# Sending each token's row to its two experts alone in a fused attention and mixture-of-experts kernel

## The chip, the cores and the metric

The kernel runs on one core of one Trainium2 chip. The metric is the device time of one execution in microseconds (us), the median of three runs; lower is better. One further execution was recorded by the hardware profiler, and all durations of single instructions come from that one. The engines are TensorE (PE in the profile; its weight loads are PEld), VectorE (DVE), ScalarE (ACT), GpSimd (POOL) and SyncE (SP). SP only issues transfers; GpSimd issues some too.

## The reference

One transformer layer on x of 2 x 2048 tokens by 512 features, in float32: attention with 16 query heads of 32 and a single key and value head, a residual and a layer norm; then a mixture of 8 experts of which each token uses 2, a residual and a layer norm.

```python
q, k, v = split(x @ Wqkv.T + b)              # q: 16 heads of 32; k and v: one head of 32
scores = q @ k.T / sqrt(32), causal mask     # 2048 x 2048 per head and batch
ctx = softmax(scores) @ v
x1 = layernorm(x + ctx @ Wout.T + b_out)

s = x1 @ router_w.T                          # 8 scores for a token
top, sel = top_k(s, 2);  g = softmax(top)    # two experts, two shares
h = silu(x1_bf16 @ w1[sel]) * (x1_bf16 @ w3[sel])     # 512 -> 128, for the two chosen
out = layernorm(x1 + sum over the two of g * (h @ w2[sel]))   # 128 -> 512
```

## The kernel before, in words

**Tiles and stages.** The 4096 tokens are 32 tiles of 128, in 8 groups of 4 tiles (`TG`), 16 tiles for each batch row. `project` turns the four x tiles of a group on TensorE, makes keys and values (`keys`) and queries (`queries`) in float32. `attention` goes through the tiles in turn; a tile T has as many steps as there are key tiles up to and with its own: 1 to 16, 272 in all. Each step is one score block, four matmuls of 512 columns into the PSUM tile `three` and one loose bank; ACT takes the exponential into `pT` (into `acc` for the tile's own, diagonal block); TensorE multiplies by the values into `cs` (`weigh`); and VectorE adds `pT` to `acc` for the softmax sums (`add_up`). The diagonal block is masked by GpSimd (`affine_select` in `exponentials`) before `weigh` uses it as its second block. `after` ends a tile: sums, the output projection with `woT`, the residual `xr` and a layer norm, of which VectorE does the statistics and GpSimd three small operations (`layernorm`, L692).

**Experts.** `experts` (L781) treats four tiles of a group together, except in the last group, whose tiles go alone. For each tile `route` turns x1 on TensorE and casts it to bf16 on GpSimd (`x1b`); `gates` makes the scores, the two best by `max` and `max_index`, and a gate of 8 numbers per token, zero but for two. Then every token goes through all eight experts: `up` and `half` do 8 matmuls each of 512 columns against `w1_sb` and `w3_sb` (in two halves of four experts), ACT takes a tanh, VectorE a product, GpSimd multiplies by the gate, VectorE multiplies into `h`; a transposing DMA on SP's queue turns `h` into `hT`; `down` does 8 matmuls of 512 columns against `w2_sb`. So a tile has 24 matmuls of 512 columns in bf16. The sum is added to x1, normalized and stored.

**What sets the order.** A planner in the kernel (`Order`, L65 on) runs when the program is built. Every piece of work is a `step` with an engine, an assumed duration, a list of buffers that it takes, marks that it waits for, and a priority or a due time. `run` picks, for the engine that can start first, the step of least priority number; scores have 0, `weigh` 1, and steps with a `Due` run at 2 or more until their due time nears. The instructions are then written in the planned order, and on the chip each engine goes through its own list in order, waiting on semaphores. Where real durations differ from the assumed ones, an engine waits at the head of its list. GpSimd's list holds the masks, the residual's bias, the layer norms and the gate products; SP's the loads of x for `project` (`xg`) and for the residual (`xr`), the transposes and the stores.

**Buffers.** Each kind of tile has a ring of its own: 3 `pT`, 2 `acc`, 4 groups of x1 (`X1B`), 2 each of `a`, `h`, `hT`, `xr`, `c_sb`, 1 each of `lT`, `ctxT`. Four loose PSUM banks serve all other matmuls.

**The end.** After all tiles a flag is read: if a softmax sum is out of bounds, the whole computation is done again by a safer form (`run(True)`). With these inputs the flag is 0.

Of the kernel before, what the change touches and what calls it, by code (L numbers as in the profile page):

```python
# [28 lines left out]
X1B = 4  # L29
# [5 lines left out]
BANK = "m"  # L35

# [23 lines left out]
class Order:  # L60
# [5 lines left out]
    LOOK = {DVE: 1.0}  # L66
    CAP = 3.0

    def __init__(self, banks, **rings):
        self.rings = {name: [n, []] for name, n in rings.items()}  # L70
        self.banks = [None] * banks
        self.busy = {e: 0.0 for e in self.LAT}
        self.sig = {}
        self.parked = []
        self.now = self.end = 0.0
        self.event = 0
        self.count = 0
        self.dues = []
        self.held = {}
# [23 lines left out]
    def hold(self, ring, n):  # L103
        self.held[ring] = [self.take(ring) for _ in range(n)]
# [6 lines left out]
    def take_all(self, rings, t):  # L111
        slots = self.slots(rings.count(BANK), t)
        tokens = []
        for ring in rings:
            if ring == BANK:
                token = Token(ring)
                token.slot = slots.pop(0)
                self.banks[token.slot] = token
# [5 lines left out]
    def slots(self, n, t):  # L124

        free = [i for i, k in enumerate(self.banks) if k is None or k.at is not None and k.at <= t + 1e-6]
        free.sort(key=lambda i: self.banks[i].at if self.banks[i] else 0.0)
        return free[:n]

    def room(self, rings):  # L130

        at = 0.0
        n = rings.count(BANK)
        if n:
            free = sorted(0.0 if k is None else k.at for k in self.banks if k is None or k.at is not None)
            if len(free) < n:
                return None
            at = free[n - 1]
        for i, ring in enumerate(rings):
            if ring == BANK:  # L140
                continue
# [30 lines left out]
    def run(self):  # L172
        while self.parked:
# [23 lines left out]
            if eng in self.LOOK and best[1][0].us > 1.0 and self.prio(best[1][0], urgent) > -0.9:  # L197

                for x in able:
                    s = x[1][0]  # L200
                    if (
                        s.eng == eng and self.prio(s, urgent) <= -0.9 and x[0] < t0 + self.LOOK[eng]
# [31 lines left out]
def mqa_postln_moe_postln(  # L234
# [22 lines left out]
    EB = 4  # L257
    scale = 1.0 / math.sqrt(HD)
# [26 lines left out]
    )  # L285
    warm = const.tile([P, 1], F32, name="warm")
# [17 lines left out]

    def run(full):
# [5 lines left out]
        n_x1 = X1B - full  # L311
        x1p = es.enter_context(tc.tile_pool(name="x1p", bufs=n_x1))
        att = es.enter_context(tc.tile_pool(name="att", bufs=1))
        ptp = es.enter_context(tc.tile_pool(name="pt", bufs=3))
# [5 lines left out]
        if full:  # L320
# [19 lines left out]

        order = Order(
            NB, three=1, pT=3, acc=2, cs=1, c_sb=2, lT=1, ctxT=1, shT=3 if full else NSH, pmax=2, xg=1, xT=1,
            xr=2, qT=2, kv=GPB + 1, x1=n_x1, x1b=1, x1T=TG, a=2, h=2, hT=2,
# [18 lines left out]
        banks = [psm.tile([P, GT], F32, name=f"bank{i}") for i in range(NB)]  # L362

        def bank(m, dtype=F32, shape=(P, GT)):
            ap = banks[m.slot][:, :]
# [10 lines left out]
        def score_banks(ms):  # L376

            if len(ms) == NG:
                of = [heads(bank(m)) for m in ms]
                return of, [([m], slice(g, g + 1), of[g][:, None]) for g, m in enumerate(ms)]  # L380
# [9 lines left out]
        def load_weights():  # L390
            nat["wkv"] = ffn.tile([2 * HD, D], F32, tag="a", name="wkv_n")
            nat["wq"] = grp.tile([P, NHH, D], F32, tag="qT", name="wq_n", bufs=2)
            nat["wo"] = grp.tile([P, NHH, D], F32, tag="qT", name="wo_n", bufs=2)
            nat["wr"] = ffn.tile([E, D], F32, tag="a", name="wr_n")
            b_row = nat["b"] = ffn.tile([1, D + 2 * HD], F32, tag="x1T", name="b_row", bufs=TG)
# [7 lines left out]
        def turn_biases():  # L403
# [23 lines left out]
            free(order.held["x1T"][0])  # L427
# [45 lines left out]


        kT, v, qTs, kv_held, qT_held, st_x = {}, {}, {}, {}, {}, {}

        def load_x(G):
            b, gi = divmod(G, GPB)
            xg = grp.tile([P, TG, D], F32, tag="xg", name="xg")
            for t in range(TG):  # L480
                s0 = gi * GT + t * P
                nc.sync.dma_start(xg[:, t, :], x[b, s0 : s0 + P, :])
            return xg

        def project(G, due):
            hurry = -1.5 if G == 0 else None
            due = Due(due, 21.7)
            (hx,) = yield step(SP, 0.0, ["xg"])
            xg = load_x(G)
            st = {}  # L490

            def turn(t):
# [737 lines left out]
```

The helper that records every operation has one line, L230, so most rows of the profile carry that line and are told apart by the names of their tiles.

## Time and profile before

| | us |
|---|---|
| median of three runs | 1216.54 |
| the three runs | 1216.75, 1216.47, 1216.54 |
| the profiled execution: its own time | 1216.7 |
| its span, first to last instruction | 1214.9 |
| VectorE's adds acc<-acc,pT (238) | 549.3 |
| ACT's exponentials pT<-three (240) | 370.1 |
| GpSimd's gate products a<-a,gt (56) | 121.4 |
| granted TensorE clock, mean | 0.992 of full |

"Busy" is the time in which at least one instruction of an engine ran. Matmuls are pipelined, so the mean duration of one is longer than the distance to the next. In a row of a group stand the line, the engine, the operation, output<-inputs by tile names, the shapes, the count, the busy time and the mean of one in ns, then the idle time of that engine just before them and what ended it. A float32 matmul shows as two records. Engine queues that issue transfers are named SPq or POOLq.

### The profile page before, as it was taken

To read this page: it belongs to the slowest core of one execution; us is meant where nothing else is said; L and a number is where in the kernel's file an instruction comes from. 1 tells how busy PE (TensorE), PEld (TensorE's weight loads), DVE (VectorE), ACT (ScalarE), POOL (GpSimd) and SP (SyncE) were. 2 spreads that over 40 slices of the span, in tenths; PEclk is the share of its full clock that TensorE was granted. 3 is DMA by queue.
4 is the path that set the end of the run, shared out by engine and by line. 5 is a ranking of instruction groups with operands and counts; after the bars stand their busy time and mean duration, and the time that the engine had idled before them with its cause. 6 is when DMAs were issued, how large, how long until landed. Compare 5 with 4: busy or idle time off the path is not lost. (4 is left out here: it accounts for less than half of the span.)

```text
span 1214.9 us, 16833 instructions
## 1 busy us (share of the span) xinstructions
PE 1151.1 (95%) x6774; PEld 370.4 (30%) x6774; DVE 910.7 (75%) x1107; ACT 696.2 (57%) x777; POOL 601.5 (50%) x355
## 2 busy tenths in 40 slices
PE   8999999999999999989999999999899899999984
PEld 5433223323222332222333223222232232232341
DVE  2348777778777898787738867868799788879774
ACT  2445666657665676556535666666657567566420
POOL 3244533424363654567544545432765687467542
PEclk9999999999999999999999999999999999999998
DMA  9201001001100201100001000000010010010121
GB/s 248 69 10 52 10 9 44 10 9 44 27 9 24 64 10 27 36 26 18 28 18 60 27 9 18 9 10 9 18 44 28 18 44 19 26 36 18 36 44 56
DMA packets 57354, 40.13 MB, mean 33 GB/s; under 512 B 42729, under 2 KB 43753, under 8 KB 57266
## 3 DMA queue, kind: packets, MB, share of 16 engines
q1 hardware_dynamic: 47248, 34.63, 10.2%
q0 software_dynamic: 9360, 3.15, 2.3%
q8 instruction: 55, 0.90, 0.3%
q10 hardware_dynamic: 658, 1.18, 0.3%
q14 instruction: 33, 0.27, 0.1%
HBM read 25.58 MB, written 8.39 MB: 28 GB/s over the span
## 5 line engine op out<-in xcount | busy, mean ns | idle before, releaser
L230 DVE TENSOR_TENSOR acc<-acc,pT 128x2048 f32<-128x2048 f32 x238 | 549.3, 2308 | 43.5 <-PE cs L230 30.4
L230 ACT ACTIVATE pT<-three,bias 128x1536 f32<-128x1536 f32 x240 | 370.1, 1542 | 325.1 <-PE bank L230 282.3
L230 PE MATMUL bank<-qT,kT_g 32*128 32x512 f32 (+1 forms) x672 | 319.2, 596 | 6.0 <-DVE h L230 4.8
L230 PE MATMUL three<-qT,kT_g 32*128 32x512 f32 x1632 | 310.2, 643 | 10.0 <-ACT pT L230 8.2
L230 POOL TENSOR_SCALAR r<-mv 128x1 f32<-128x1 f32 x64 | 82.5, 1288 | 407.6 <-DVE mv L230 403.7
L230 PE MATMUL cs<-pT,v_g 128*32 128x512 f32 x1920 | 257.9, 608 | 0.2 <-ACT pT L230 0.2
L230 POOL TENSOR_TENSOR a<-a,gt 128x512 f32<-128x512 f32 x56 | 121.4, 2171 | 97.9 <-DVE a L230 97.8
L230 POOL TENSOR_SCALAR x<-x,mv,r 128x512 f32<-128x512 f32 x62 | 166.5, 2685 | 6.8
L230 ACT ACTIVATE pT<-bank,bias 128x512 f32<-128x512 f32 x240 | 163.5, 681 | 0.6 <-PE bank L230 0.6
L230 PE MATMUL bank<-w_sb,x1b 128*128 128x512 bf16 x512 | 125.7, 382 | 9.0 <-DVE h L230 8.2
L230 PEld LDWEIGHTS three<-qT,kT_g 32*128 32x128 f32 x1632 | 83.2, 183 | 163.6 <-ACT pT L230 86.1
L230 PE MATMUL bank<-xT,wqT 128*128 128x512 f32 x256 | 129.2, 621 | 0.0
L230 PE MATMUL bank<-woT,ctxT 128*128 128x512 f32 x256 | 126.1, 613 | 2.5 <-DVE ctxT L230 2.5
L230 POOL TENSOR_SCALAR_AFFINE_SELECT acc<-acc 128x2048 f32<-128x2048 f32 x32 | 68.6, 2145 | 72.1 <-ACT acc L230 72.1
L230 PEld LDWEIGHTS cs<-pT,v_g 128*32 128x32 f32 x1920 | 38.2, 108 | 174.7 <-issue 168.8
L230 POOL TENSOR_TENSOR r<-r,neg_half 128x1 f32<-128x1 f32 x64 | 86.1, 1345 | 5.3
L230 ACT ACTIVATE acc<-three,bias 128x1536 f32<-128x1536 f32 x32 | 49.4, 1543 | 67.8 <-PE three L230 44.4
L230 DVE TENSOR_TENSOR h<-bank,a 128x512 bf16<-128x512 f32 x56 | 38.6, 690 | 59.6 <-POOL a L230 59.6
L230 PEld LDWEIGHTS bank<-qT,kT_g 32*128 32x128 f32 x544 | 79.7, 183 | 8.1 <-DVE h L230 4.1
L230 PEld LDWEIGHTS <-x1b 128*128 128x128 bf16 x512 | 45.5, 98 | 108.0 <-issue 62.0
L230 PE MATMUL bank<-w_sb,hT 128*128 128x512 bf16 x256 | 64.3, 387 | 5.1 <-DMA hT<-h 4.7
L230 PEld LDWEIGHTS bank<-woT,ctxT 128*128 128x128 f32 x256 | 44.2, 189 | 78.8 <-issue 64.7
(109 smaller groups left out, 931.9 us busy)
## 6 DMA issues: line engine op xcount, KB each, us to landing
xg<-in_L_attn_x_dram SPq DMA_DIRECT2D x32, 256.0 KB, 3.8
xr<-in_L_attn_x_dram SPq DMA_DIRECT2D x32, 256.0 KB, 2.7
out_dram<-x SPq DMA_DIRECT2D x32, 256.0 KB, 2.0
w_sb<-in_L_ffn_w_dram POOLq DMA_DIRECT2D x8, 256.0 KB, 8.9
wq_n<-in_L_attn_Wqkv_w_dram ACTq DMA_DIRECT2D x4, 256.0 KB, 6.0
wo_n<-in_L_attn_out_w_dram SPq DMA_DIRECT2D x1, 1024.0 KB
w_sb<-in_L_ffn_w_dram POOLq DMA_DIRECT2D x1, 1024.0 KB, 14.9
hT<-h SPq DMA_TRANSPOSE x31, 3.0
```

Source lines behind the costliest of these rows:

```text
L230: return lambda *a, **k: self.tc.keep_in_program_order(getattr(self.engine, name)(*a, **k))
```

## The change

Seven of the eight groups leave the dense expert block. Their tokens are taken in four sets (two groups, two groups, two groups, one group). For each set there is room in DRAM for 448 rows per expert (256 in the last set).

- `choose(G)` scores a group's tokens as before, then counts with matmuls against ones and a triangle which place each token has in the list of each of its two experts, and writes places and shares.
- `scatter(T)`: two indexed DMAs from GpSimd's queue write a tile's 128 normalized rows, cast to bf16, to their places in `x_by`. Places never written hold zeros, filled at the start by four DMAs from the same queue.
- `expert_set`: for each expert a transposing DMA on SP loads its 448 (or 256) rows; `expert` multiplies with the weights as the fixed operand and the tokens as the moving one; `down` multiplies blocks of 128 rows by `w2_sb`, ACT copies the result out of PSUM and SP stores it in `y_by`.
- `combine` and `second`: x1 is loaded back from DRAM, two indexed DMAs on GpSimd's queue gather each token's two rows of y, VectorE adds them with their shares, and the layer norm follows.
- The last entry of each set in `SETS` gives the attention steps between which the set's experts are planned.
- The last group keeps the dense block, tile by tile.
- Many rings become one pool of 20 pages of 128 x 512 float32 (`PAGES`), with a limit for each kind; `pT` has 5 buffers in place of 3; x of the projection is loaded tile by tile; the four loose banks are one PSUM tile.
- The planner may keep TensorE from starting a lesser step of over 0.5 us if a score step could start within 0.25 us (`LOOK`).
- The flag also covers the counts: if an expert has more tokens than its room, the whole is done again by the safer form, which is dense.

```diff
-X1B = 4
+PAGES = 20
+PT = 5
+X1 = 6
+SETS = (
+    ((0, 1), (448,), (59, 149)), ((2, 3), (448,), (150, 202)), ((4, 5), (448,), (190, 241)),
+    ((6,), (256,), (227, 264)),
+)
...
-    LOOK = {DVE: 1.0}
+    LOOK = {DVE: 1.0, PE: 0.25}
...
+            first_ = 0.0 if eng == PE else -0.9
+            if eng in self.LOOK and best[1][0].us > (0.5 if eng == PE else 1.0) and self.prio(best[1][0], urgent) > -0.9:
...
+                        s.eng == eng and (s.prio == 0.0 if eng == PE else self.prio(s, urgent) <= -0.9) and x[0] < t0 + self.LOOK[eng]
...
+    x_by = [dram.tile([E * n, D], BF16, name=f"x_by{i}") for i, n in enumerate(room)]
+    y_by = [dram.tile([E * n, D], F32, name=f"y_by{i}") for i, n in enumerate(room)]
+    x1_d = dram.tile([NT * P, D], F32, name="x1_d")
...
-        ptp = es.enter_context(tc.tile_pool(name="pt", bufs=3))
+        ptp = es.enter_context(tc.tile_pool(name="pt", bufs=3 if full else PT))
...
         order = Order(
-            NB, three=1, pT=3, acc=2, cs=1, c_sb=2, lT=1, ctxT=1, shT=3 if full else NSH, pmax=2, xg=1, xT=1,
-            xr=2, qT=2, kv=GPB + 1, x1=n_x1, x1b=1, x1T=TG, a=2, h=2, hT=2,
+            NB, PAGES, dict(
+                x1=n_x1, xg=TG, xr=2, lT=1, ctxT=1, c_sb=2, x1T=TG, a=2, h=2, hT=2, y=4, back=9,
+            ),
+            three=1, pT=3 if full else PT, acc=2, cs=1, shT=3 if full else NSH, pmax=2, xT=1,
+            qT=2, kv=GPB + 1, x1b=2, hc=2,
         )
...
             gps.dma_start(w2_sb, w2.rearrange("e p d -> p e d"))
+            for places_ in x_by:
+                k = places_.shape[0] // P
+                gps.dma_start(
+                    places_[:, :].rearrange("(p k) d -> p k d", p=P),
+                    zeros[:, None, :].to_broadcast([P, k, D]),
+                )
...
             mark("ln", T)
             alone = G == NGRP - 1
-            if alone or t == TG - 1:
+            if G in set_of and not full:
+                yield step(SP, 0.0)
+                nc.sync.dma_start(x1_d[T * P : (T + 1) * P, :], y)
+                if t == TG - 1:
+                    spawn(choose(G))
+            elif alone or t == TG - 1:
...
+        def choose(G):
...
+            (m,) = yield step(PE, 0.5, ["m"], due=due)
+            p_n = bank(m, F32, (P, TG + 1, E))
+            flat = p_n.rearrange("p t e -> p (t e)")
+            mm(
+                p_n[:, : TG + 1, :], ones_b, both[:, TG, None, :].to_broadcast([P, TG + 1, E]),
+                start=True, stop=False,
+            )
+            for t in range(TG):
+                mm(
+                    p_n[:, t + 1 :, :], ones_b,
+                    both[:, t, None, :].to_broadcast([P, TG - t, E]), start=False, stop=False,
+                )
+            mm(flat[:, : TG * E], tri, both[:, :TG, :].rearrange("p t e -> p (t e)"), start=False, stop=True)
+            yield step(DVE, 1.7)
...
+            for t in range(TG):
+                spawn(scatter(Ts[t]))
...
+        def scatter(T):
+            i_set = set_of[T // TG]
+            for k in range(2):
+                yield step(POOL, 1.2)
+                ins = gps.indirect_dma_start(
+                    out=x_by[i_set][:, :], out_offset=place(T, k), in_=x1s[T], in_offset=None,
+                    bounds_check=E * room[i_set] - 1, oob_is_err=False,
+                )
...
+            yield step(SP, 0.0, lat=3.0)
+            free(x1_held[T])
+            mark("there", T)
+
+        def expert_set(i_set, between):
...
+                    (h_x,) = yield step(
+                        SP, 0.0, ["x1b"], after=[("there", T) for T in Ts] + [("scores", now)]
+                    )
+                    xT = ffn.tile([P, NDC, n], BF16, tag="x1b", name="xbT", bufs=2)
+                    got = nc.sync.dma_start_transpose(xT, x_by[i_set][at_ : at_ + n, :])
...
+                    spawn(expert(i_set, e, at_, n, xT, h_x, due))
+                    at_ += n
+            spawn(combine(i_set, Ts))
+
+        def expert(i_set, e, at_, n, xT, h_x, due):
+            yield step(SP, 0.0, lat=4.5)
...
+            m, h_a = yield step(PE, us, ["m", "a"], due=due)
+            p1 = bank(m, F32, (P, n))
+            for dc in range(NDC):
+                mm(p1, w1_sb[:, dc, e, :], xT[:, dc, :], start=(dc == 0), stop=(dc == NDC - 1))
+            spawn(other())
+            yield step(ACT, 0.2 + 0.4 * n / GT)
+            a = page(h_a, (n,))
+            act.activation(a, p1, AF.Tanh, scale=0.5)
+            yield step(DVE, 0.1 + 0.6 * n / GT)
+            vec.scalar_tensor_tensor(a, a, 1.0, p1, ALU.add, ALU.mult)
...
+            vec.tensor_mul(h, st["p3"], a)
...
+        def down(i_set, e, at_, h, due, h_h):
+            m, h_y = yield step(PE, 0.25, ["m", "y"], due=due)
...
+            mm(p_y, h, w2_sb[:, e, :], start=True, stop=True)
...
+            yield step(ACT, 0.6)
+            y = page(h_y)
+            act.copy(y[:rows, :], p_y)
...
+            nc.sync.dma_start(y_by[i_set][at_ : at_ + rows, :], y[:rows, :])
...
+        def combine(i_set, Ts):
...
+            for T in Ts:
+                h_x, *h_g = yield step(SP, 0.0, ["back"] * 3)
+                y = page(h_x)
+                nc.sync.dma_start(y, x1_d[T * P : (T + 1) * P, :])
+                parts = []
+                for k in range(2):
+                    yield step(POOL, 1.2)
+                    part = page(h_g[k])
+                    gps.indirect_dma_start(
+                        out=part, out_offset=None, in_=y_by[i_set][:, :], in_offset=place(T, k),
+                        bounds_check=E * room[i_set] - 1, oob_is_err=False,
+                    )
+                    parts.append(part)
+                spawn(second(T, y, h_x, parts, h_g))
+
+        def second(T, y, h_x, parts, h_g):
+            b, i = divmod(T, TPB)
+            yield step(SP, 0.0, lat=3.0)
+            for k in range(2):
+                yield step(DVE, 0.7 + 0.95 * k)
+                vec.scalar_tensor_tensor(y, parts[k], shares[:, k, T : T + 1], y, ALU.mult, ALU.add)
+                free(h_g[k])
+            yield from layernorm(y)
+            yield step(SP, 0.0)
+            nc.sync.dma_start(out[b, i * P : (i + 1) * P, :], y)
```

The numbers in `step` are the planner's assumptions in us, written into the kernel; they are no measurements.

## The prediction

> **What bounds the kernel now.** I read the busy shares, the stretches of 100 us, the groups of instructions by shape, the order of time on TensorE, and last the waits. Busy time over the whole span:
>
> ```profile
> PE 1151.1 (95%) x6774; PEld 370.4 (30%) x6774; DVE 910.7 (75%) x1107; ACT 696.2 (57%) x777; POOL 601.5 (50%) x355
> ```
>
> TensorE is the bound in the mean. It stands idle for 1214.9 - 1151.1 = 64 us. The stretches (us; busy time of PE, PEld, DVE, ACT and POOL, each with its instructions; clock; DMA) say where:
>
> ```profile
> 200.00:300.00 100.00, 99.23 (x611) 30.31 (x611) 77.86 (x83) 65.88 (x74) 40.13 (x19) 1.00 0.09 30
> 500.00:600.00 100.00, 92.68 (x570) 29.29 (x573) 80.64 (x100) 57.07 (x64) 63.50 (x34) 0.98 0.09 24
> 900.00:1000.00 100.00, 92.36 (x603) 29.57 (x602) 88.88 (x99) 61.89 (x70) 72.19 (x37) 1.00 0.12 32
> 1100.00:1215.00 115.00, 90.27 (x479) 33.52 (x478) 82.76 (x197) 38.32 (x53) 49.91 (x42) 0.94 0.16 38
> ```
>
> Attention without experts fills TensorE to 99%. Where the expert block joins in, VectorE (DVE) rises to 89% and GpSimd (POOL) to 72%, and TensorE falls to 92%: from there on three engines are close together. The groups that the change touches or leans on:
>
> ```profile
> L230 DVE TENSOR_TENSOR acc<-acc,pT 128x2048 f32<-128x2048 f32 x238 | 549.3, 2308 | 43.5 <-PE cs L230 30.4 <-ACT pT L230 4.8 <-DVE acc L230 0.5
> L230 PE MATMUL bank<-w_sb,x1b 128*128 128x512 bf16 x512 | 125.7, 382 | 9.0 <-DVE h L230 8.2 <-DVE a L230 0.8
> L230 PE MATMUL bank<-w_sb,hT 128*128 128x512 bf16 x256 | 64.3, 387 | 5.1 <-DMA hT<-h 4.7
> L230 POOL TENSOR_SCALAR x<-x,mv,r 128x512 f32<-128x512 f32 x62 | 166.5, 2685 | 6.8
> L230 POOL TENSOR_TENSOR r<-r,neg_half 128x1 f32<-128x1 f32 x64 | 86.1, 1345 | 5.3
> L230 POOL DMA_DIRECT2D w_sb<-in_L_ffn_w_dram x9 | 8.2, 933 | 0.4 <-POOL w_sb L230 0.3
> ```
>
> The means of the matmuls overlap, so they are no price; the time from start to start is (start, duration, operation):
>
> ```profile
> 1082.98 1.90 PE L230 MATMUL bank<-w_sb,hT 128*128 128x512 bf16 x8
> 1084.81 0.70 PE L230 MATMUL three<-qT,kT_g 32*128 32x512 f32 x3
> ```
>
> Eight expert matmuls of 512 columns take 1.83 us: 0.229 each.
>
> **TensorE: what is removed and added.** In 28 of 32 tiles the dense block goes: 28 x 24 = 672 matmuls of 512 columns. In their place stand 192 of 448 columns, 64 of 256 and 112 of 512 (the last block of a 448 has 64 rows but still moves 512 columns). In columns that is 159,744, or 312 matmuls of 512, so 360 are saved: 82.4 us. The counting adds 42 small matmuls; the nearest row is a bf16 weight load of 98 ns, so 4 us. Net -78 us; by the other reading of the expert rows (188.07 us busy for all 768, 0.245 each) it is -84. The Trainium skill, page "TensorE: Matmul & The Clock Gate", section "Back-to-back issue gap", gives N/2.4 + 2.5 ns, so 216 ns for 512 columns; by it the saving is some 4 us less. Transposes, router and all attention matmuls keep their number, and the four-bank form of the scores is in neither program's order. "TensorE holds back" is no instruction, only another order: nothing, and its cover is that a score matmul follows at once; without it, it costs the 0.25 us that it looks ahead. The third to fifth pT buffers I also put at nothing; at most they save the 10.0 us that the group of "three" matmuls waited for ACT.
>
> **VectorE.** Gone: 56 h multiplies (0.690), 56 of 64 full a products (0.677, eight stay), 28 adds of x (0.684) and the gate chain (7 us): 103 us. Added: products and multiplies on 448 and 256 columns (35 us by columns), 56 "part times share plus y" (nearest row 0.68: 38 us) and 7 counting chains of some 12 short operations (rows 0.16 to 0.22: 14 us). So -15 us in all, to about 896. But it moves: the first set's results are combined after tile 19, the second's about tiles 26 and 27, the third's at tiles 29 to 31. In the order of the changed program, between the last adds of tiles 28 and 31 VectorE has 40 adds (92 us), some 20 combining products, 15 normalizations, the last dense tiles and the last experts, 155 us at these rows. TensorE has 138 us there. At the 89% that is VectorE's fullest stretch above, 155 becomes 174; TensorE's 138 at the ratio of this trace, 1214.9 us over 1117 summed from the same prices, becomes 150. So VectorE takes the bound there: +20 us (bounds 0, if more pT buffers let it run full, and 24).
>
> **ACT.** Tanh shrinks by some 18 us, but 112 copies of y out of PSUM (nearest row 0.597) add 66: 744 us, 64%. It stays under the rest: nothing; its cover is the 36% left.
>
> **GpSimd, the price that no row shows.** Gone are the gate product (121.4) and the bf16 cast (24.6). Added are 56 scatters and 56 gathers of 128 rows. The floor is the 0.933 us of a weight load's issue, taken while VectorE was idle. Against it stands this row of small operations (min/median/max ns):
>
> ```profile
> L230 POOL TENSOR_SCALAR r<-mv x64: 223/2013/2375, 57.5 to 1205.9; 128x1 f32<-128x1 f32 x64
> L230 POOL TENSOR_TENSOR r<-r,neg_half x64: 568/570/2685, 57.8 to 1206.2; 128x1 f32<-128x1 f32 x64
> ```
>
> They are 0.2 and 0.6 us long, yet often 2.1 longer: about one VectorE add of 2.308. Over r, pow, x and the gate product the mean lies 0.9 above the minimum, so I take 0.93 + 0.87 = 1.8 us; the ends are 0.93 and 3.0 (every issue waits out an add). The Trainium skill, page "DMA: Bandwidth & Descriptors", section "SWDGE vs HWDGE vs iDMA", speaks against the change: GpSimd builds these descriptors in rings in SBUF, which VectorE locks it out of in a two-port mode. If that held each time, every issue would sit at the upper end; no run here shows it yet.
>
> Who waits: GpSimd works in order, and behind the indexed transfers stands each tile's causal mask, for which cs<-acc on TensorE waits, in order too. Normalizing one tile costs 1.288 + 1.345 + 2.685 = 5.3 us, an x residual 1.44, a mask 2.15. Counted in the changed order:
> - Masks of tiles 20 to 24: 32 transfers, 14 normalizations, 5 residuals, 5 masks: 32c + 92. TensorE has 123, stretched 134; another 10 us lie between a tile's own scores and the use of its mask. At c = 1.8: +6.
> - Tile 28: 6c + 46 against 47 + 10: 0.
> - Tiles 30 and 31: 24c + 71 against 98 + 10: +6, under VectorE's 20, so 0.
>
> **SP and the transfers.** Added: 32 transposed loads, 112 stores of y, 28 stores and 28 loads of x1; removed: 28 hT transposes. The row:
>
> ```profile
> L954 SPq DMA_TRANSPOSE hT<-h x31: 1231/1232/1754, 315.7 to 1197.7; - x31
> DMA to landing us min/median/max: 3.0/3.0/4.8
> ```
>
> A load of 448 x 512 is 1.75 times as large: 2.2 us of issue, 5.3 to land. The first load of a set waits on SP for all the set's scatters, with stores and the next xr behind it. But by the order TensorE has 10 to 70 us of other work between what frees a load's buffer and its first use, three near the end 4.6 us. So nothing; without that cover 32 x 5.3. Traffic: 40 MB plus some 82 is 106 GB/s, against 248 in the page's first slice. At the start four fills of zeros (13.1 MB, 12,800 rows) stand on GpSimd between weight loads and the first masks: at 0.933 per 1024 runs 12 us of issue, most of it in the 21 us that GpSimd idled before its first mask; +4, bounds 0 and 12.
>
> **Sum**, against the profiled 1216.7 us (span 1214.9): -78 + 20 + 6 + 4, and -4 for half of the 9.0 us that the w_sb group waited for VectorE: -52, so **1165 us**. The median of the runs shown is 0.2 lower.
>
> **The rivals.**
> - *All of the saving stays* (0.27): scatters near 0.93, the buffers keep VectorE full. For it: 99% TensorE in plain attention. Against: the 92% beside 89%. -84 - 8 + 2: 1127 us.
> - *GpSimd becomes the bound, slower* (0.14): the place is the masks of tiles 20 to 24 and 30 to 31. At c = 3.0 the three stages give 44, 7 and 35 (15 beyond VectorE's 20): -78 + 20 + 66 + 12 is 1237 us. The excess is 62c - 120, and it eats the saving from c = 2.8 on. For it: the median of r<-mv; against: x and pow are mostly at their minimum.
> - *Loads land late* (0.06): if eight loads and the first gathers of four sets each cost their 5.3 us, the forecast becomes 1165 + 64 = 1229, or 1190 at half of that, slower only if all do. Against: the work in between.
> - *The counting overflows and the full fallback runs* (0.01): more than double. By the reference's inputs the fullest expert holds 394 of 448 places and 196 of 256.
>
> **How the numbers follow.** The forecast has 0.52, with its own range 1143 to 1190. The range 1122 to 1218 holds the first rival and leaves out the upper ends. Faster by over 0.2% (about what a measurement of this kernel can tell from no change): 0.52 + 0.27 and half of the late loads, 0.82. Slower: the second rival and the rest, 0.15.
>
> **What would show it.** Right: expert matmuls (408 of 512 columns left) down to about 100 us busy, TensorE over 96% up to 500 us, VectorE over 90% in the last 150 us of scores. GpSimd's issue of the indexed transfers near 1.8 us would prove my price; above 2.8, with TensorE waiting for acc from GpSimd for tens of us, the second rival. PE waiting for xbT would prove late loads. A span under 1135 would make the VectorE stage wrong.

## The result and the profile after

| | us | ratio to before, 95% interval |
|---|---|---|
| before, median of 5 runs | 1216.54 (1213.22 to 1219.05) | |
| after, median of 5 runs | 1620.65 (1617.07 to 1640.51) | 1.3362 [1.3322, 1.3401] |
| forecast | 1165 (range 1122 to 1218) | |
| after, profiled execution (the highest of the five) | 1640.51, span 1638.8 | |

The kernel is a third slower. In the runs below, one execution of e4 (5705.35 us) and two of e13 (2552.44 and 1516.96 us) took far longer than the others of the same program; the medians hold them, the ratios do not, and without them e4 is at 1173.00 and e13 at 1219.09 us.

The page after, its busy shares and two rows of its 40 slices:

```profile
PE 1344.6 (82%) x6485; PEld 418.6 (26%) x6512; DVE 905.1 (55%) x1138; ACT 762.0 (46%) x865; POOL 577.2 (35%) x390
...
PE   6788999899998999877878788878888878757963
...
PEclk9789999899999999989799799998998979878976
```

TensorE has fewer matmuls to do and is busy 194 us *longer* than before (1151.1). VectorE and ACT did about what the prediction counted (896 and 744 us), GpSimd less than before (601.5), but in 424 us more. So no engine was given that much work: TensorE's own instructions stretched, and it stood idle for 294 us. The stretches that answer to those of before (us; busy time of PE, PEld, DVE, ACT and POOL, each with its instructions; clock; DMA):

```profile
200.00:300.00 100.00, 90.03 (x475) 27.09 (x473) 59.26 (x79) 48.63 (x53) 39.73 (x23) 0.97 0.15 38
500.00:600.00 100.00, 94.19 (x496) 27.05 (x495) 60.81 (x70) 57.75 (x59) 30.24 (x18) 1.00 0.12 27
900.00:1000.00 100.00, 80.61 (x332) 24.00 (x334) 56.16 (x90) 40.77 (x46) 55.46 (x41) 0.91 0.34 90
```

From 200 to 300 us there is next to no expert work, in either kernel: before, the first expert matmul starts at 294.51 us, and after at 443.26; the stretch after holds only some counting and the first scatters (from 224.8 us). Before, TensorE did 611 instructions there; now it does 475 and still counts as 90% busy. So the loss is not in the expert matmuls. The waits after (engine and tile, who ended the wait, us in total, times, longest):

```profile
ACT pT L263 <- PE loose L263: 260.1, 169, 13.6
DVE page L263 <- PE loose L263: 249.0, 66, 16.7
...
ACT page L263 <- PE loose L263: 137.7, 89, 11.5
```

`loose` is the tile that now holds all four loose banks. Two rows of the waits before, to compare:

```profile
ACT pT L230 <- PE bank L230: 282.9, 189, 4.5
...
DVE x L230 <- PE bank L230: 49.9, 20, 5.6
```

ACT stood idle for its next score before as well, and for longer, so its first row proves nothing by itself. VectorE's wait has grown: `page` now stands for several tiles of before, but x, the one that waited longest for a bank, came to 49.9 us. What each instruction waits for is seen in the order of time. The order of time on TensorE after (start, duration, operation, count):

```profile
604.93 1.07 PE L263 MATMUL cs<-pT,v_g 128*32 128x512 f32 x8
605.93 1.12 PE L263 MATMUL loose<-xT,wqT 128*128 128x512 f32 x2
606.98 1.13 PE L263 MATMUL three<-qT,kT_g 32*128 32x512 f32 x6
607.83 1.12 PE L263 MATMUL loose<-qT,kT_g 32*128 32x512 f32 x2
608.88 1.06 PE L263 MATMUL cs<-pT,v_g 128*32 128x512 f32 x8
```

And on ACT in the same stretch (in brackets the idle time before and who ended it):

```profile
603.14 0.69 ACT L263 ACTIVATE pT<-loose,bias 128x512 f32<-128x512 f32 x1 [1.26 <-PE loose L263]
...
607.09 0.69 ACT L263 ACTIVATE pT<-loose,bias 128x512 f32<-128x512 f32 x1 [1.26 <-PE loose L263]
```

Before, the same score block looked so:

```profile
604.42 0.70 PE L230 MATMUL three<-qT,kT_g 32*128 32x512 f32 x3
604.44 0.69 PE L230 MATMUL bank<-qT,kT_g 32*128 32x512 f32 x1
604.95 0.60 PE L230 MATMUL three<-qT,kT_g 32*128 32x512 f32 x3
604.97 0.59 PE L230 MATMUL bank<-qT,kT_g 32*128 32x512 f32 x1
```

Read the two together. Before, the four matmuls of a score (two records each) run side by side: from 604.42 to the next matmul at 605.49, 1.07 us. After, three run together for 0.85 us (606.98 to 607.83), and the fourth, into `loose`, runs by itself for 1.05 us: 1.90 us. ACT says why. The exponential out of the loose bank was written by the score at 603.88, but it starts at 607.09, when the projection's matmul into *another* bank (605.93) has ended. It ends at 607.78, and only then, at 607.83, does the fourth matmul start, into another bank again. So ACT waits for the last write into any bank, and TensorE for the last read of any bank.

The built programs show the same without any time. Of the instructions of ACT and VectorE that read PSUM and carry a wait for TensorE, 955 of 956 before wait for the very matmul that wrote what they read. After, 226 of 750 do; the others wait for one that stands 1 to 35 matmuls later.

### The profile page after: what moved, and what is told of

It reads as the page before. It is cut to its first block, busy times and chain, and to the rows that moved or that the text cites. A ratio compares the mean times of both kernels' runs of the same rounds, so it can differ in the third digit from the quotient of the medians.

```text
span 1638.8 us, 17050 instructions
## 1 busy us (share of the span) xinstructions
PE 1344.6 (82%) x6485; PEld 418.6 (26%) x6512; DVE 905.1 (55%) x1138; ACT 762.0 (46%) x865; POOL 577.2 (35%) x390
## 5 line engine op out<-in xcount | busy, mean ns | idle before, releaser
L263 PE MATMUL loose<-qT,kT_g 32*128 32x512 f32 (+1 forms) x672 | 335.1, 624 | 18.4 <-ACT page L263 5.8
L263 ACT ACTIVATE pT<-loose,bias 128x512 f32<-128x512 f32 x240 | 165.4, 689 | 294.3 <-PE loose L263 243.3
L263 PE MATMUL loose<-woT,page 128*128 128x512 f32 x256 | 147.0, 685 | 26.6 <-ACT page L263 7.6
L263 PE MATMUL loose<-xT,wqT 128*128 128x512 f32 x256 | 140.9, 664 | 22.7 <-ACT pT L263 5.6
L263 POOL TENSOR_SCALAR page<-page,mv,r 128x512 f32<-128x512 f32 x62 | 155.8, 2512 | 6.7
L263 ACT COPY page<-loose 128x512 f32<-128x512 f32 (+2 forms) x145 | 82.0, 589 | 133.3 <-PE loose L263 109.4
L263 DVE TENSOR_TENSOR page<-loose,page 128x512 f32<-128x512 f32 x36 | 24.9, 691 | 162.3 <-PE loose L263 133.0
L263 PEld LDWEIGHTS loose<-qT,kT_g 32*128 32x128 f32 x544 | 83.9, 192 | 108.7 <-ACT pT L263 63.4
L263 POOL DMA_INDIRECT page<-y_by,places x56 | 76.3, 1363 | 50.9 <-ACT pT L263 17.7
L263 POOL DMA_INDIRECT x_by<-page,places x56 | 83.0, 1483 | 28.3 <-issue 15.2
L263 PE MATMUL loose<-xbT,w_sb 128*128 128x448 bf16 (+1 forms) x256 | 59.5, 364 | 31.3 <-ACT page L263 13.4
```

The lines of the kernel that those rows point to most:

```text
L263: return lambda *a, **k: self.tc.keep_in_program_order(getattr(self.engine, name)(*a, **k))
```

## The experiments

Ratios are to the kernel before, run on the same chip, with 95% intervals. "Theory" and "rival" are names that the expectations give to the explanations that a run can tell apart.

| run | us | ratio |
|---|---|---|
| e1, changed, banks apart | 1236.41 | 1.0179 [1.0156, 1.0202] |
| e2, before, banks as one tile | 1697.61 | 1.395 [1.3927, 1.3974] |
| e3, e1 with GpSimd's real prices | 1227.47 | 1.0105 [1.0078, 1.0132] |
| e4, e1 without indexed transfers | 1173.18 | 0.9645 [0.9612, 0.9678] |
| e5, e1 without holding back | 1265.91 | 1.0425 [1.0392, 1.0458] |
| e6, e1 with 3 pT | 1241.14 | 1.021 [1.0181, 1.0239] |
| e7, e1 with plain gathers | 1183.48 | 0.9731 [0.9704, 0.9759] |
| e8, e3, normalizations on ACT | 1226.49 | 1.0095 [1.0062, 1.0128] |
| e9, before, with holding back | 1238.6 | 1.0192 [1.0165, 1.0219] |
| e10, e1 with plain gathers, same order | 1182.01 | 0.972 [0.9686, 0.9754] |
| e11, e3, combining spread | 1213.07 | 0.9982 [0.9963, 1.0001] |
| e12, e11, earlier windows | 1218.37 | 1.0025 [1.0005, 1.0045] |
| e13, e10 with dummy operations | 1220.76 | 1.0038 [1.0021, 1.0055] |
| e14, e11, gathers planned later | 1212.46 | 0.9982 [0.996, 1.0004] |
| e15, e14, second normalizations on ACT | 1188.16 | 0.9769 [0.9741, 0.9797] |
| e16, e15, first ones too | 1188.53 | 0.9793 [0.9767, 0.982] |
| e17, e15, earlier windows | 1201.45 | 0.9891 [0.9867, 0.9915] |

### e1 and e2: the four banks as one tile

The hunk that the prediction did not cost, taken back:

```diff
-        loose = psm.tile([P, NB, GT], F32, name="loose")
-        banks = [loose[:, i, :] for i in range(NB)]
+        banks = [psm.tile([P, GT], F32, name=f"bank{i}") for i in range(NB)]
...
             if len(ms) == NG:
-                ms = sorted(ms, key=lambda m: m.slot)
-                all_ = loose.rearrange("p g (h k) -> p g h k", h=NHH)
-                return [all_[:, g] for g in range(NG)], [
-                    (ms[: NG - 1], slice(0, NG - 1), all_[:, : NG - 1]),
-                    (ms[NG - 1 :], slice(NG - 1, NG), all_[:, NG - 1 :]),
-                ]
+                of = [heads(bank(m)) for m in ms]
+                return of, [([m], slice(g, g + 1), of[g][:, None]) for g, m in enumerate(ms)]
```

> The changed kernel, with the four loose PSUM banks as four tiles again (as before the change) and all else as changed; the order of instructions on each engine is the same, only waits differ. Theory W (whole-tile waits: with the four banks as one tile, a reader of one bank waits for the last matmul into any bank, and a matmul into one bank waits for the last reader of any bank): the waits of ACT for PE on the loose banks, 260 us for pT, and of VectorE, 249 us, fall back to the size of before; the score's fourth matmul starts with the other three again (four in about 1.07 us instead of 1.9); the time falls from 1620 to 1130 to 1200 us, near what the prediction's sum gave without this wait. Rival G (GpSimd, DMA traffic and VectorE's combining hold TensorE back, and the waits on the banks only pass that on): at most 60 us are won, the time stays above 1550 us. Rival L (the shared pages or the TensorE look-ahead spoil the order): the time stays above 1450 us.

Measured: 1236.41 us. The built programs have the same instructions, in the same order on TensorE, ACT and VectorE (on GpSimd's and SP's lists some neighbours change places); the waits differ. So the one tile cost 1620.65 - 1236.41 = 384 us. The four matmuls of a score take 1.07 us again (896.89 to 897.96), and VectorE's wait for banks fell from 249.0 to 89.3 us. The same stretches again:

```profile
200.00:300.00 100.00, 98.89 (x649) 28.87 (x648) 86.13 (x89) 72.66 (x79) 43.26 (x22) 1.00 0.20 47
500.00:600.00 100.00, 100.00 (x577) 34.24 (x577) 67.30 (x102) 65.57 (x86) 36.46 (x28) 1.00 0.43 109
900.00:1000.00 100.00, 82.50 (x537) 24.64 (x535) 76.01 (x89) 68.52 (x86) 52.28 (x29) 0.93 0.37 104
```

The first two are full. In the third TensorE still lacks 17.5 us of 100. The expectation of 1130 to 1200 was missed: something else is left, some 70 us above the forecast.

e2 puts the one tile into the kernel before and changes nothing else.

> The kernel before, with its four loose banks made one PSUM tile and nothing else; the same order of instructions. Theory W: the time rises from 1217 to 1500 to 1700 us, with scores of about 1.9 us where the bank is waited for. Rivals G and L: within 2% of 1217 us, since neither indexed transfers nor pages are in it.

Measured: 1697.61 us, 481 us over before. So the tile alone does it, without experts by places, pages or scatters. Its mark is TensorE waiting, in front of a bank, for an exponential, a wait that the kernel before does not have at all:

```profile
PE loose L230 <- ACT pT L230: 132.2, 147, 2.5
```

### e3 to e6: what is left over

Where TensorE waited in e1:

```profile
PE bank L263 <- POOL page L263: 27.8, 3, 11.5
PE cs L263 <- POOL acc L263: 19.2, 8, 5.3
PE bank L263 <- DMA xbT<-x_by: 18.9, 2, 12.3
PE bank L263 <- DVE page L263: 12.0, 7, 3.3
```

GpSimd heads the list twice: pages that it normalizes, and masks. Before, the mask wait was 5.3 us. e3 and e4 ask what makes GpSimd late; e5 and e6 take back two other parts of the change.

e3, the planner's prices for GpSimd as the profile shows them:

```diff
-            yield step(POOL, 0.5 if last else 2.0, prio=-1.0)
+            yield step(POOL, 0.5 if last else 4.7, prio=-1.0)
-            yield step(POOL, 1.6, lat=3.0)
+            yield step(POOL, 1.9, lat=3.0)
-                yield step(POOL, 2.05, prio=-2.0)
+                yield step(POOL, 2.3, prio=-2.0)
```

(and 1.9 and 1.6 instead of 1.2 for a scatter and a gather)

> The program with four banks apart (1236.4 us), and in its planner GpSimd's steps at about what the profile shows: a normalization 4.7 us instead of 2.0, a mask 2.3 instead of 2.05, a residual 1.9 instead of 1.6, an indexed scatter 1.9 and a gather 1.6 instead of 1.2. Only the order of instructions changes. Theory O (GpSimd's list is ordered by prices that are too low, so masks and normalizations stand behind work that is not ready, and TensorE waits 28 us for pages from GpSimd and 19 us for masked blocks): these two waits fall below 20 us in all, and the time to 1190 to 1215 us. Theory I (the indexed transfers themselves and the barrier at the end of each set cost the time, in any order): 1225 to 1245 us.

Measured 1227.47 us, 9 us less, in the range of theory I: a better order exists, but the prices are not the cause.

e4, no indexed transfer:

```diff
                 for k in range(2):
-                    yield step(POOL, 1.2)
                     part = page(h_g[k])
-                    gps.indirect_dma_start(
-                        out=part, out_offset=None, in_=y_by[i_set][:, :], in_offset=place(T, k),
...
+                    nc.sync.dma_start(part, y_by[i_set][k * P : (k + 1) * P, :])
```

(and the two scatters of each tile left out)

> The program with four banks apart (1236.4 us), with the 56 scatters left out (the experts multiply the zeros of the start fills) and the 56 gathers replaced by plain loads of 128 rows on SP's queue, so that GpSimd issues no indexed transfer; all other work stays. The output lacks the experts' contribution for seven groups. Theory I (163.6 us of issue on GpSimd and what stands behind them): 1150 to 1180 us, with TensorE's waits for GpSimd below 20 us. Theory O (GpSimd's list waits for VectorE's statistics in order, 339 us idle there, whether or not transfers stand in it): 1210 to 1240 us.

Measured 1173.18 us: 63 us less, inside what theory I expected. TensorE's waits for GpSimd came to 19.8 us. The planner made another order without these steps, though, so the 63 us are not the transfers' alone.

e5, without the rule by which TensorE holds back:

```diff
-    LOOK = {DVE: 1.0, PE: 0.25}
+    LOOK = {DVE: 1.0}
```

> The program with four banks apart (1236.4 us), without the rule that TensorE holds back for a score (the planner's look-ahead for VectorE stays). Prediction's step (it is only another order, worth nothing): within 6 us of 1236. Rival (the holding back leaves gaps that cost): at least 10 us faster.

Measured 1265.91 us, 30 us *more*: a miss for both. e9 below asks whether the rule is good in itself.

e6, `PT = 3`:

> The program with four banks apart (1236.4 us), with 3 buffers pT in place of 5. Prediction's step (worth nothing, at most 10 us): 1230 to 1247 us. Rival (five buffers are what lets VectorE lag by several blocks while the experts run): over 1250 us.

Measured 1241.14 us, 5 us more, with overlapping intervals: as predicted, next to nothing.

### e7 to e10: scatters, gathers, order

e7 is the e4 diff for the gathers alone.

> The program with four banks apart (1236.4 us), with only the 56 gathers replaced by plain loads of 128 rows on SP's queue; the scatters stay. The seven groups' output takes wrong rows of y. Leaving out both kinds brought 63 us. If the gathers carry it (they stand together at the end of each set, before masks and normalizations): 1175 to 1200 us. If the scatters do (1.65 us of issue each against 1.27, and the experts' loads wait for them): 1212 to 1236 us. If each costs by its issue (92 and 71 us): near 1209.

Measured 1183.48 us: the gathers carry 53 of the 63 us, though their issue is the shorter of the two.

e8 moves the end of every normalization but the last tile's from GpSimd to ACT, on top of e3:

```diff
-            (vec if last else gps).tensor_scalar(y, y, mv[:, 0:1], r, ALU.subtract, ALU.mult)
+            nb = sml.tile([P, 1], F32, tag="nb", name="nb")
+            gps.tensor_scalar(nb, mv[:, 0:1], r, -1.0, ALU.mult, ALU.mult)
+            yield step(ACT, 0.7, prio=-0.5)
+            act.activation(y, y, AF.Identity, bias=nb, scale=r)
```

> The program with four banks apart and GpSimd's prices as measured (1227.5 us), with the last operation of the normalizations (2.76 us on GpSimd, 62 times) as an activation with scale and bias on ACT, and one more small operation of 128x1 on GpSimd. If GpSimd's load in the expert stages is what the indexed transfers made too large, this takes 171 - 40 us from it and the time falls to 1165 to 1200 us. If the in-order waits for VectorE's statistics are what counts, whatever GpSimd does after them: 1215 to 1230 us. If ACT (some 40 us more) delays exponentials: above 1230 us.

Measured 1226.49 us, the same as e3. This looks like a vote against GpSimd's load, but the waits show that the queue only moved:

```profile
PE three L263 <- ACT pT L263: 52.9, 24, 10.4
PE bank L263 <- ACT page L263: 19.1, 9, 7.2
...
ACT page L263 <- POOL nb L263: 104.2, 36, 11.9
```

In e3, which it builds on, the first of these was 12.3 us. ACT goes through its list in order too: where a normalization waits at its head for GpSimd (104.2 us in all, for the small tile `nb`), exponentials stand behind it.

e9, the rule of e5 added to the kernel before (the same lines of `run` and `LOOK` as in the change):

> The program of before with only the rule that TensorE holds back for a score (0.25 us). Without that rule the changed program with banks apart lost 30 us. Prediction's step (another order, worth nothing): 1210 to 1222 us. Rival (the rule brings what it brought there, in any program): 1185 to 1205 us.

Measured 1238.6 us, 22 us more, outside both expectations. So one and the same rule brings 30 us in one program and costs 22 in the other. Both runs only change the order, and show how much an order can be worth here: some 20 to 30 us either way. Differences of that size between programs of different order, from e3 on, prove no cause by themselves.

That made e7 doubtful, since leaving the gathers out also changed the planner's order. e10 keeps `yield step(POOL, 1.2)`, so the order of TensorE, ACT and VectorE stays that of e1:

```diff
                     yield step(POOL, 1.2)
                     part = page(h_g[k])
-                    gps.indirect_dma_start(
...
+                    nc.sync.dma_start(part, y_by[i_set][k * P : (k + 1) * P, :])
```

> The program with four banks apart (1236.4 us), with the 56 gathers replaced by plain loads on SP's queue, but planned as if they still stood on GpSimd, so that TensorE, VectorE, ACT and GpSimd keep their order of instructions and GpSimd's list loses the gathers alone. The output takes wrong rows of y. Theory G (the gathers' issue, 71 us in bursts of eight tiles ahead of masks and normalizations, is what cost the 53 us that the run without them gained): 1180 to 1200 us. Theory R (most of the 53 us came from the other order that the planner made without them): 1215 to 1235 us.

Measured 1182.01 us: 54 us less in the same order. It is the gathers, their waits included: a plain load waits only for the stores of the rows that it reads, a gather for all of its set's. How they act is seen in e1 at the end of a set, in the chain that ended last (start, duration, operation):

```profile
904.16 4.63 POOL page L263
...
909.75 3.95 POOL page L263
...
914.68 2.59 POOL r L263
...
917.37 3.83 POOL page L263
...
921.20 0.20 POOL r L263
921.40 0.16 SPq L1089
...
922.13 4.11 DMA xbT<-x_by
```

and what TensorE does meanwhile:

```profile
913.28 0.72 PE L263 MATMUL bank<-w_sb,hc 128*128 128x512 bf16 x2
926.28 1.67 PE L263 MATMUL bank<-xbT,w_sb 128*128 128x448 bf16 x4 [12.28 <-DMA xbT<-x_by]
```

After a set's last store, the gathers and normalizations of its eight tiles come to GpSimd all at once. In e1 GpSimd worked 42.75 of the 50 us from 850 on. Its normalizations run late, and SP's queue, in order as well, has a store of a normalized tile (L1089) ahead of the next set's transposed load. The load goes out at 922.13 when the store is let go, and TensorE stands for 12.28 us.

### e11 to e17: the burst, and what relieves it

e11 starts combining tile by tile, on top of e3:

```diff
+GAP = (6, 4, 3, 2)
...
-            for T in Ts:
-                h_x, *h_g = yield step(SP, 0.0, ["back"] * 3)
+            first_, gap = SETS[i_set][2][1], GAP[i_set]
+            for n, T in enumerate(Ts):
+                h_x, *h_g = yield step(
+                    SP, 0.0, ["back"] * 3, after=[("scores", min(first_ + gap * n, U[-1] - 1))]
+                )
```

> The program with four banks apart and GpSimd's prices as measured (1227.5 us), with the combining of a set's tiles started one tile every 6, 4, 3 and 2 attention steps from the set's end on, and not all at once. Every computation stays. Theory G (the cost is the burst of gathers and normalizations after each set, about 8 x 7.4 us on GpSimd at once): 1180 to 1205 us. Theory R (order alone, up or down 25 us whatever is moved) or the load in total: 1210 to 1245 us.

> The same with spread combining, and the sets' windows of attention steps earlier (50 to 125, 145 to 190, 182 to 225, 222 to 256), so that less combining is left for the last 100 us, where TensorE was busy 68% of the time. Theory G: 10 to 25 us under the run with spread combining alone. Rival (the experts' loads then wait for their scatters): 5 to 20 us over it.

Measured 1213.07 us for e11, 14 us under e3. That is in the range of theory R, not of G: spreading the burst brings, at most, a quarter of what the gathers cost, and the order changed with it. e12 gave 1218.37 us: the rival's sign.

e13 puts work in the gathers' places of e10 that waits for nothing:

```diff
+                    gps.tensor_add(idle, idle, bo_sb)
```

> The run with plain gathers in the same order (1182.0 us), and in each gather's place in GpSimd's list an addition of 128x512 into a tile that nobody reads (1.3 to 1.8 us, as long as a gather's issue with its gap, 1.6 us), which waits for no transfer and no page. Theory W (the gathers cost by waiting at the head of GpSimd's list for the stores of y and for their pages, 37 us and one of 22 us, with masks and normalizations behind): 1180 to 1195 us. Theory O (they cost by the time that they take from GpSimd in the bursts): 1215 to 1240 us.

Measured 1220.76 us. By 1219.09 us, 37 of the 54 us came back with no gather in the list. So GpSimd's *time* is a large part of the price. How large stays open: the dummies took 101.6 us, more than the gathers' 71.4, and VectorE's busy time rose from 906.9 to 933.5 us beside them. In proportion to 71.4 us, 26 of the 54 would be time (an estimate). TensorE's waits tell the same: those for pages, masks and transposed loads sum to 65.9 us in e1, 24.9 in e10 and 45.8 in e13. Five stretches of 50 us with much combining (600 to 700, 850 to 950, 1050 to 1100 us) show the exchange; they are the same times, not exactly the same work, and e15, told below, has another order:

| busy in these 250 us | GpSimd | TensorE |
|---|---|---|
| e1 | 194.9 | 197.5 |
| e13 | 206.8 | 210.3 |
| e10 | 158.3 | 230.7 |
| e15 | 154.1 | 230.2 |

e14 leaves the work and plans gathers 8 us later and the reuse of stored pages 12 us after the store:

> The run with spread combining (1213.1 us), and in the planner 8 us more between a set's last store of y and its first gather, and 12 us in place of 2.5 until a stored page is free again. Only the order changes. Theory W: the waits of gathers (86 us idle before them) fall by half or more, and the time to 1190 to 1206 us. Theory O: 1206 to 1220 us.

Measured 1212.46 us, no change against e11. But the waits that it was to halve rose, from 86.0 us in front of the gathers in e11 to 110.3 here:

```profile
L264 POOL DMA_INDIRECT page<-y_by,places x56 | 81.9, 1462 | 86.0 <-DMA y_by<-page 27.3 <-ACT pT L264 27.2 <-DMA out_dram<-page 13.7
L264 POOL DMA_INDIRECT page<-y_by,places x56 | 79.6, 1421 | 110.3 <-DMA y_by<-page 52.5 <-ACT pT L264 15.8 <-DVE bias L264 9.4
```

(e11, then e14). So the condition of theory W was not met, and the run does not decide; that more waiting cost nothing speaks against W, weakly. e15 then takes time off GpSimd: in `second` alone, the normalization ends on ACT as in e8, but with `lat=12.0` in the planner, so that ACT comes to it late.

> The last one, and the last operation of the 28 normalizations after combining on ACT, planned 12 us after GpSimd's part, so that ACT should not wait for it (with all normalizations there ACT waited, and TensorE 53 us for pT). Theory O (time taken from GpSimd): 28 x 2.8 = 78 us less on GpSimd, 20 to 40 us under the last one. Theory W: within 10 us of it.

Measured 1188.16 us, 24 us under e14 and 28 under the kernel before: faster than both, with every computation in place. GpSimd's busy time fell from 603.2 to 564.0 us, half of the 78 expected, while the gathers still had 92.5 us of idle time in front of them. That fits theory O; it does not prove it, since the order changed too and 24 us is what an order alone was worth in e5 and e9. Its waits on ACT stay small:

```profile
PE cs L264 <- POOL acc L264: 22.4, 7, 6.8
PE three L264 <- ACT pT L264: 13.3, 17, 1.7
```

> The run with spread combining and the second normalizations on ACT (1188.2 us), with the first normalizations of the seven groups ended on ACT too, planned 8 us after GpSimd's part. Theory O (time taken from GpSimd): some 28 x 2.2 us less on GpSimd, TensorE's 22 us of waits for masked blocks fall to 10 or less, 1170 to 1185 us. Rival (ACT waits in order for late statistics, with exponentials behind, as when all went there without the distance): over 1192 us.

> The run with spread combining and the second normalizations on ACT (1188.2 us), with the sets' windows of attention steps earlier (50 to 125, 145 to 190, 182 to 225, 222 to 256). TensorE is busy 55% in its last 86 us. If combining left for the end holds it up: 1175 to 1186 us; if the windows only move the same work (as in the run before, +5 us): 1186 to 1196 us.

e16 gave 1188.53 us, no more gain, and between its two expectations: TensorE's wait for masked blocks was still 18.3 us, its wait for pT 17.3. e17 gave 1201.45 us, 13 us more and outside both of its expectations; why earlier windows cost so much there was not looked into. What holds e15 at 1188 is open too.

## Why the prediction was wrong, point by point

With the runs the measured time can be laid out along the sum, one part of the change after the other. e4 has another order than e1, so the two middle rows can shift against each other by the 20 to 30 us that an order is worth. The prediction's terms without GpSimd's give 1216.7 - 78 + 20 + 4 - 4 = 1159 us.

| | us | from |
|---|---|---|
| the sum without GpSimd's term | 1159 | prediction |
| what the other terms missed | +14 | e4, 1173.18 |
| the indexed transfers; the term was +6 | +63 | e1 - e4 |
| four banks as one tile; no term | +384 | after - e1 |
| after | 1620 | 1620.65 |

- **The step that failed is the one that was not made.** The part by part costing spoke of the four loose banks only as "the four-bank form of the scores is in neither program's order" and so put that edit at nothing, without a price, a cover or a rival for the rest of it. That form is indeed in neither order. But making four tiles one also changed what every user of a bank waits for, with no instruction added: 384 of the 404 us, shown by e1 and, from the other side, by e2. The waits of the program stand in it before any run.
- **GpSimd's term was 6 and measured 63 us with e4, 54 of them in an unchanged order (e10), though its price was too high.** An issue took 1.48 us (scatter) and 1.36 us (gather) in the profile after, 1.65 and 1.27 in e1, where 1.8 was taken. What failed is the comparison of whole stages ("32c + 92" against "134 + 10"). Within a stage the work comes in bursts, and the next mask, page or store is needed before the burst is through, as at the end of a set in e1. By e13 some 26 to 37 of the 54 us are time taken from GpSimd; what the rest is, waiting or the transfers themselves, is not shown.
- **TensorE's -78 held, to within 10 us.** The six groups of expert matmuls of e1 sum to 118 us busy, from 190.0 before: -72 in busy time ("about 100" was too low). Without indexed transfers (e4) TensorE's total was 1082.0, 69 under before.
- **VectorE as the bound at the end (+20) was not reached.** In e1 VectorE was busy 86% from 1100 to 1215 us and 68% in the 100 us before, not over 90%. The term can't be separated by these runs: the 1159 us hold its 20, and the 14 us that were missed hold what was wrong with it and with everything else, the shared pages among them, which were not tried apart.
- **ACT nothing, pT nothing:** right (735.5 us in e1; e6).
- **"TensorE holds back" nothing:** wrong in size, and of no fixed sign: -30 us (e5) and +22 us (e9).
- **SP and the loads:** a transposed load landed after a median 4.2 us, where 5.3 was estimated, and took 1.5 us of issue, not 2.2. "Nothing" was still wrong with the banks apart: 18.9 us of TensorE's waits in e1 are for such loads, held up as shown above. That is the place of the third rival, at a third of its price.
- **The start (+4):** the zero fills took 5.8 us of issue, not 12.
- **The second rival** named 1237 us and masks that come late. With the banks apart the time was 1236, and the transfers on GpSimd's list were the largest part of what was missing. But its condition, c from 2.8 on, was not met; the two numbers agree by chance.

The page "DMA: Bandwidth & Descriptors" of the Trainium skill, which the prediction weighed (section "SWDGE vs HWDGE vs iDMA"), says that VectorE in a two-port mode locks GpSimd out of the rings into which it writes descriptors. The 56 scatters after took 0.99 us at the least, 1.01 in the median and 2.96 at the most: some issues were stretched, but not each. That it was this lock that stretched them, no run here shows.

## What to carry to other kernels

When a diff changes how buffers are cut into tiles, compare what each reader and writer waits for before counting instructions: one tile for four independently used banks cost 384 us here, and 481 in the kernel before, without a single instruction more. Off the bound engine, compare work with time in the stretch between a burst's arrival and its first deadline, not in whole stages. And put a moved operation into another in-order list only behind enough distance that it never waits at the head.

## What the runs showed of the hardware

Where the fourth of a score's four matmuls of 32 rows is held back, the other three still run together, but the fourth then costs about what all four cost together: 1.05 us against 1.07.

After a long wait TensorE's clock is lower for some microseconds. In e1 it waited 11.49 us for a page up to 645.47 us; stretches of 5 us around it, busy PE first and the granted clock third from the end:

```profile
630.00:635.00 5.00, 3.74 (x30) 1.67 (x28) 4.97 (x4) 3.17 (x6) 4.81 (x4) 1.00 0.20 55
635.00:640.00 5.00, 0.00 (x0) 0.00 (x0) 4.90 (x5) 1.67 (x3) 4.79 (x3) 0.59 0.38 117
640.00:645.00 5.00, 0.00 (x0) 0.00 (x0) 4.86 (x7) 0.00 (x0) 4.81 (x3) 0.50 0.10 40
645.00:650.00 5.00, 4.53 (x14) 1.42 (x14) 0.30 (x1) 0.59 (x1) 4.46 (x5) 0.54 0.45 157
650.00:655.00 5.00, 5.00 (x66) 1.84 (x65) 0.00 (x0) 2.19 (x3) 3.40 (x4) 1.00 0.54 177
```

The clock falls to half while TensorE idles and stays there for most of the first 5 us of work. After the 12.28 us wait shown above, four matmuls of 448 columns took 1.67 us; the four that started at 930.72 took 0.93. So a long wait costs some 2 us beyond itself (an estimate: 4.53 us of work at 0.54 of the clock). The Trainium skill, "TensorE: Matmul & The Clock Gate", section "What's actually happening", gives half clock after an idle window of about 3.4 us and full clock after as long of work. On the restart the rows agree: 0.54 from 645 to 650 us is half clock for all but some 0.4 us. On the fall they do not quite: 0.59 from 635 to 640 us is full clock for 0.9 us, so the clock fell at about 635.9, some 1.9 us after the wait began at 633.98.
